# A Perceiver kernel's first cross attention: GpSimd's order within a key unit, values given out by half chunks, and scales spread at the end of the loop

## The chip, the cores and the metric

The kernel runs on one core of one Trainium2 chip (trn2). Its time is the device time of one execution in microseconds (us). Runs of one kernel are summed up by their median.

Engines are named as in the profile: PE is TensorE (matmul; PEld its weight loads), DVE is VectorE, ACT is ScalarE, POOL is GpSimd, SP is SyncE, which here only issues DMA transfers. An "L221" is line 221 of the kernel. Most instructions of the stage at issue carry that line, because a helper issues them, so they are told apart by the names of their tiles.

## The reference: what is computed

The reference is a network of four levels with twelve layers, each of the form `x = x + layer(layernorm(x))`, on `x` of 2 batches x 128 tokens x 256 channels. Only the first layer matters here, and of the tenth (the fourth level's cross attention) one tile pool. The first layer is a cross attention with int8-like fake quantisation:

```
q = layernorm(x) @ Wq + bq                  # 16 heads of 16 channels
k, v = split(ctx @ Wkv + bkv)               # ctx: 4096 tokens x 256 channels
q, k: quantised per token and head, scale = max|.| / 127
v: quantised per channel, scale = max|.| / 127 over all tokens
weights = softmax(q k^T / 4), quantised per row, scale = max / 255
x = x + (weights @ v) @ Wp + bp
```

The context of 4096 tokens is shared by both batches. In the kernel's code the softmax's weights are rounded to int16 by the conversion of an exponential, whose bias holds the maximum and log 255, and the row sums (`z`) divide the output at the end.

## The kernel before, in words

One program runs the twelve layers one after the other. The change concerns `l0_xattn` (from L316), which has a preparation and a loop. All its compute instructions go through `InOrder` (L213 to L221), which keeps each engine's instructions in the order in which the program names them. So the order of the work is written by hand: an engine never starts an instruction before those named earlier for it, and an instruction that waits holds up all behind it on its engine. DMA instructions stand in the queue of the engine that issues them.

**Loads.** ScalarE issues the loads of the key and value weights (`wkv`, one transfer), the query weights, the biases, and the output weights (L351 to L363); SyncE issues eight chunks of 512 context tokens, transposed (`ctxT`).

**Preparation** (a loop of ten steps `s`). Context tokens are 32 tiles of 128. Keys are made in eight units of four tiles (`Keys`). For a unit:

- `projected(0)` and `projected(2)`: TensorE projects two tiles each; VectorE adds the bias into `kn`.
- `scaled`: VectorE takes the maximum per token and head and the scale's reciprocal (`tr`, `kqr`); GpSimd multiplies `kn` by `kqr`. In the profile this is `kn<-kn,kqr`.
- `quantised`: ScalarE rounds to int16 (`kw<-kn`), VectorE multiplies by the scale (`kn<-kw,tr`).
- `first`: ScalarE casts the result to bf16 in the first third of `kpad`; GpSimd subtracts this part from `kn` (`kn<-kn,kpad`).
- `second`: ScalarE casts what is left to bf16 in the second third.
- `third`: GpSimd subtracts that too (`kpad<-kn,kpad`, the last third), and SyncE issues a DMA transpose of the unit's `kpad` into `kT` (L443).

So GpSimd has three operations for a unit: scaling, first, third. In step `s` the unit `s-2` does `second` and `third`, then unit `s-1` does `quantised` and `first`, then unit `s` does `scaled`. GpSimd's order in a step is therefore third(s-2), first(s-1), scaled(s).

Values are made transposed, in two halves of 128 channels (`Values(c)`), each in four chunks `n` of 1024 tokens, each of two half chunks `j`. TensorE projects a half chunk; ScalarE adds the bias and writes it to `vf` (`vf<-mm,bv`). VectorE takes the chunk's largest magnitude (`m<-vf`); after the fourth chunk the half's scale and its reciprocal (`vs`, `vr`) are known. `rounded(n)`: ScalarE rounds the chunk to int16 in `vws[n]`; `turned_values`: VectorE turns it into bf16 in place (`vw<-vw`), and SyncE issues a DMA transpose into `vi` (L347). There are four `vws` tiles, used by half 0 and again by half 1. One chunk is projected in each of steps 0 to 7: its first half chunk is copied out at once, its second in the next step (`late`).

`queries(b)` (ten VectorE instructions on small tiles and one transpose into `qT`) runs in steps 1 and 2 for the two batches.

**Loop** (`Round(h, b)`: 16 heads x 2 batches = 32 rounds). `scores(k)`: two matmuls of 512 keys into one of three PSUM tiles `sc`, from which VectorE copies to `S` with a running maximum (`S<-sc`). `weights`: VectorE makes the bias `nb`, ScalarE the rounded exponentials `Si` with their row sums (`Si<-S,nb,sq`), SyncE a DMA transpose into `pT`. `output(k)`: 8 matmuls into `po`, four rounds later (`LAG` = 4), so that in each turn of the loop TensorE does scores(k) of round n and output(k) of round n-4 by turns. There are two `S`, three `Si` and four `pT` tiles. The last round's exponentials are made in quarters, and its transposes are done on TensorE (`turned`, PSUM tiles `sc`, VectorE copies `pT<-sc`) rather than by DMA.

Before the loop, rounds 0 and 1 do scores 0 to 2; then half 1's values are turned; the bias `bp` is added to `x`; and the two rounds do scores 3 (which need `kT` of the last two units) and weights. Then `spread` of each half: VectorE makes a diagonal matrix of the value scales (`dg`), TensorE multiplies it with ones to give the scales in every partition (`sv`, one PSUM tile), ScalarE copies that to `svb`. `svb` is used only once, at the end, by the last product (L609).

In the tenth layer (L1333 on) the tile pool `l3kv` holds the norm weights and the tiles `kq`, `rot`, `v`. A tile pool that is opened on memory used by earlier tiles makes the first writers of its tiles wait for these; with `reuse_waits="tile"` each tile waits only for those that lay in its own place.

Of the kernel before, what the change touches and what calls it, by code (L numbers as in the profile page):

```python
# [12 lines left out]
F32 = mybir.dt.float32  # L13
# [4 lines left out]
AF = mybir.ActivationFunctionType  # L18
ALU = mybir.AluOpType
# [3 lines left out]
P = 128  # L23
B = 2
D = 256
# [290 lines left out]
def l0_xattn(g):  # L316
# [8 lines left out]
    nc, tc = g.nc, g.tc  # L325
# [3 lines left out]
    UP = 2.0 ** 64  # L329
    with ExitStack() as ctx:  # L330
        p1 = ctx.enter_context(tc.tile_pool(name="l0x", bufs=1, reuse_waits="tile"))
        pe, dve, act, pool = (InOrder(tc, e) for e in (nc.tensor, nc.vector, nc.scalar, nc.gpsimd))
# [6 lines left out]
        svb = p1.tile([P, D], F32, name="svb")  # L339
# [3 lines left out]
        def turned_values(c, n):  # L343

            vb = vws[n].bitcast(BF16)
            dve.tensor_scalar(vb, vws[n], UP, None, ALU.mult)
            nc.sync.dma_start_transpose(out=vi[:, 8 * n:8 * n + 8, c * P:(c + 1) * P], in_=vb)  # L347

        with tc.tile_pool(name="ctx0", bufs=1, reuse_waits="tile") as pc, tc.tile_pool(name="l0p", bufs=2, reuse_waits="tile") as p2, g.psum():
            ctxT = pc.tile([P, 2, NK], F32, name="ctxT0")  # L350
            wkv = pc.tile([P, 2, 2 * D], F32, name="wkv")  # L351
            nc.scalar.dma_start(wkv, g.ins["L0_xattn_Wkv"])
            wq = pc.tile([P, 2, D], F32, name="wq")
            nc.scalar.dma_start(wq, g.ins["L0_xattn_Wq"])
            bk = pc.tile([P, D], F32, name="bk")
# [1 line left out]
            bv = pc.tile([P, 2], F32, name="bv")  # L357
# [3 lines left out]
            nc.scalar.dma_start(wp, g.ins["L0_xattn_Wp"])  # L361
            bp = p1.tile([P, D], F32, name="bp")
            nc.scalar.dma_start(bp, g.ins["L0_xattn_bp"].partition_broadcast(P))  # L363
            for n in range(8):
                nc.sync.dma_start(ctxT[:, :, n * 512:(n + 1) * 512], g.ins["ctxT"][n])
            kpads = []
            for i in range(2):
# [19 lines left out]
            def queries(b):  # L387

                ps = g.acc()
                for c in range(2):  # L390
                    pe.matmul(ps, lhsT=xnT[:, c, b * P:(b + 1) * P], rhs=wq[:, c, :], start=(c == 0), stop=(c == 1))
                q = p2.tile([P, 16, 16], F32, tag="q16", name="q16", bufs=1)
                dve.tensor_tensor(q, ps.rearrange("p (h d) -> p h d", d=16), bq.rearrange("p (h d) -> p h d", d=16), ALU.add)
                dve.tensor_scalar(q, q, 0.25, None, ALU.mult)
                s, r = sq[:, b], g.sm([P, 16], "fqr")
                dve.tensor_reduce(s, q, AX.X, ALU.max, apply_absolute_value=True)
                dve.tensor_scalar(s, s, 1.0 / 127.0, 1e-8, ALU.mult, ALU.max)
                dve.reciprocal(r, s)
                dve.tensor_tensor(q, q, r.unsqueeze(2).to_broadcast([P, 16, 16]), ALU.mult)
                dve.tensor_scalar(nsq[:, b], s, -1.0, None, ALU.mult)  # L400
                for i in range(3):
                    dve.tensor_scalar(qpads[b][:, :, 16 * i:16 * i + 16], q, MAGIC, MAGIC, ALU.add, ALU.subtract)
                nc.sync.dma_start_transpose(out=qT[:, b], in_=qpads[b].rearrange("p h k -> p (h k)"))

            class Keys:
# [23 lines left out]
                def quantised(self):  # L429
# [15 lines left out]
            class Values:  # L445
# [7 lines left out]
                def projected(self, n, j):  # L453

                    if j == 0:
                        self.vf.append(p2.tile([P, 1024], F32, tag="vf", name="vf", bufs=4))
                    k0 = 1024 * n + 512 * j
                    ps = g.mm()
                    for k in range(2):
                        pe.matmul(ps, lhsT=wkv[:, k, D + self.c * P:D + (self.c + 1) * P], rhs=ctxT[:, k, k0:k0 + 512], start=(k == 0), stop=(k == 1))  # L460
                    return lambda: act.activation(self.vf[n][:, 512 * j:512 * j + 512], ps, AF.Identity, bias=bv[:, self.c:self.c + 1])

                def largest(self, n):
                    dve.tensor_reduce(self.m4[:, n:n + 1], self.vf[n], AX.X, ALU.max, apply_absolute_value=True)
# [5 lines left out]
                    dve.tensor_scalar(s, s, 1.0 / 127.0, 1e-8, ALU.mult, ALU.max)  # L470
                    dve.reciprocal(self.r, s)

                def spread(self, dg, ps):

                    dve.tensor_scalar(dg, g.ident, self.s, 2.0 ** 133 / UP, ALU.mult, ALU.mult)
                    pe.matmul(ps, lhsT=g.ones, rhs=dg, start=True, stop=True)
                    act.copy(svb[:, self.c * P:(self.c + 1) * P], ps)

                def rounded(self, n):
                    act.activation(vws[n], self.vf[n], AF.Copy, scale=self.r)  # L480

            vals, units, late = [Values(0), Values(1)], [], None

            when = {n + 4 * c: (c, n) for c in range(2) for n in range(4)}
            for s in range(8 + 2):
                now = Keys(s) if s < 8 else None
                one = units[s - 1] if 0 <= s - 1 < 8 else None
                two = units[s - 2] if s >= 2 else None
                if two:
                    two.second()  # L490
                    two.third()
                if late:
                    late()
                    late = None
                if now:
                    units.append(now)
                    now.projected(0)
                if one:
                    one.quantised()
                    one.first()  # L500
                if now:
                    now.projected(2)
                    now.scaled()
                if s - 1 in when:
                    c, n = when[s - 1]
                    vals[c].largest(n)
                if s in when:
                    c, n = when[s]
                    if c == 1:
                        vals[0].rounded(n)  # L510
                    vals[c].projected(n, 0)()
                    late = vals[c].projected(n, 1)
                    if c == 1:
                        turned_values(0, n)
                if s == 0:
                    turned_queries()
                if 1 <= s < 1 + B:
                    queries(s - 1)
            for n in range(4):
                vals[1].rounded(n)  # L520

        with tc.tile_pool(name="l0s", bufs=2, reuse_waits="tile") as p2, tc.tile_pool(name="l0ps", bufs=1, space=PSUM, reuse_waits="tile") as pp:
# [63 lines left out]
            for now in rounds:  # L586
                now.scores(3)
                now.weights(False)
            for v in vals:
                v.spread(p2.tile([P, P], F32, tag="dg", name="dg"), pp.tile([P, P], F32, tag="sv", name="sv", bufs=1))  # L590
            for n in range(2, len(todo) + LAG):
                now = Round(*todo[n]) if n < len(todo) else None
                rounds.append(now)
                if n == len(todo) + 1:
                    for k in range(4):
                        rounds[len(todo) - 1].turned(k)
                for k in range(4):
# [735 lines left out]
def l3_xattn(g, ctxT, cos, sin):  # L1333
# [10 lines left out]
    SCALE = float(np.float32(1.0 / np.sqrt(HD)))  # L1344
    pe, dve, pp = nc.tensor, nc.vector, None
    with ExitStack() as ctx:
        pk = ctx.enter_context(tc.tile_pool(name="l3kv", bufs=1))
        qw = pk.tile([P, HD], F32, name="qw")
        nc.sync.dma_start(qw, g.ins["L3_xattn_q_norm_w"].partition_broadcast(P))
        kw = pk.tile([P, HD], F32, name="kw")  # L1350
# [861 lines left out]
```

## Time and profile before

| what | us |
|---|---|
| runs of this kernel | 1601.31, 1607.47, 1612.97 |
| median | 1607.47 |
| the profiled execution's own time | 1609.98 |
| its span (first to last instruction) | 1608.3 |
| mean granted TensorE clock in the span | 0.89 |
| first matmul of the preparation | 8.60 |
| first and last scaling of a key unit on GpSimd, start | 16.62, 78.00 |
| last transpose into `kT`, issue | 88.85 |
| round 2's first `S<-sc` | 107.80 |
| last `S<-sc` of round 31, start | 258.46 |
| end of the outputs (`o<-po,z`, start) | 270.12 |

Views of the profile used below: the busy time of each engine in stretches of the span, with the clock that TensorE was granted as a share of full speed; the chain of work that ended last, followed back from the end (start, duration, engine, tile, and how many pieces were put together); the waits, by the engine that sat idle and by the work that released it (total, times, longest); and the timeline of an engine (start, duration, operation, output and inputs, and in brackets the idle time just before it with its releaser). SPq is SyncE's queue of DMA issues; the time of one issue there is how long it holds the queue, and its data land later. A line of instructions with "x8" and three durations gives the shortest, the median and the longest in ns.

### The profile page before, as it was taken

How to read it: one execution, taken by the hardware profiler on the slowest of the kernel's cores; microseconds unless marked ns; L12 is line 12 of the kernel's file. 1: busy time of each engine (PE TensorE's matmuls, PEld its weight loads, DVE VectorE, ACT ScalarE, POOL GpSimd, SP SyncE). 2: the span in 40 equal slices, each digit the busy share in tenths (PEclk: the TensorE clock that was granted, in tenths of full speed). 3: DMA queues.
4: the chain of work that ended last, by engine and by line, in shares of the span. 5: the costliest groups of instructions: out<-in, count | busy, mean ns of one | idle time of the engine just before them, and what ended most of it. 6: DMA issues, size and time to landing. Idle time of an engine off the chain costs nothing.

```text
span 1608.3 us, 17969 instructions
## 1 busy us (share of the span) xinstructions
PE 1444.2 (90%) x6732; PEld 908.3 (56%) x6732; DVE 1135.4 (71%) x1975; ACT 822.1 (51%) x1275; POOL 148.7 (9%) x140
## 2 busy tenths in 40 slices
PE   7759997898869999859999999999978999999978
PEld 5413334666546777636566566566544566666667
DVE  6869996485446476564765765765826899999976
ACT  3657775323213412315455455455546788888822
POOL 6710002020000000000000000000000111111110
PEclk9955555799979998769999999999999999999999
DMA  6889999734230430100000000000105122221110
GB/s 180 155 153 204 203 206 178 240 106 144 69 115 14 113 94 14 36 7 0 14 1 14 14 1 14 1 1 1 34 26 236 51 101 102 101 102 44 34 33 7
DMA packets 205615, 127.06 MB, mean 79 GB/s; under 512 B 177192, under 2 KB 184632, under 8 KB 202200
## 3 DMA queue, kind: packets, MB, share of 16 engines
q1 hardware_dynamic: 202720, 123.97, 30.2%
q10 hardware_dynamic: 2744, 1.76, 0.4%
q8 instruction: 53, 0.87, 0.2%
q14 instruction: 34, 0.28, 0.1%
q0 software_dynamic: 64, 0.18, 0.0%
HBM read 81.93 MB, written 0.26 MB: 51 GB/s over the span
## 4 chain that ended last, share of the span: by engine, by line
PE 73%; DVE 14%; ACT 7%; DMA 2%; issue 2%; POOL 1%; SPq 0%; ACTq 0%; DVEq 0%; POOLq 0%
PE mm L221 14%; PE wide L221 12%; PE mm L178 7%; PE py L221 7%; PE sc L221 6%; PE pb L221 6%; PE tr L221 4%; PE po L221 2%; PE acc L1147 2%; PE acc L221 2%; PE one L221 1%; DVE S L221 1%; DVE ro L221 1%; PE acc L1361 1%; DVE bc L221 1%
## 5 line engine op out<-in xcount | busy, mean ns | idle before, releaser
L221 DVE TENSOR_SCALAR_CACHE_REDUCE S<-sc 128x1024 f32<-128x1024 f32 x128 | 150.2, 1219 | 11.5 <-PE sc L221 11.0
L221 PE MATMUL py<-pT,v 128*128 128x512 f32 x272 | 142.5, 609 | 5.0 <-ACT pT L1476 4.9
L221 ACT ACTIVATE Si<-S,nb,sq 128x4096 int16<-128x4096 f32 (+1 forms) x35 | 122.7, 3506 | 46.2 <-issue 28.2
L221 PE MATMUL sc<-kT,qT 48*128 48x512 bf16 x256 | 130.6, 615 | 15.5 <-DMA kT<-kpad 6.4
L221 PE MATMUL wide<-kT,qT 128*128 128x512 f32 x256 | 120.7, 601 | 3.7 <-ACT v L1397 3.7
L1476 ACT COPY pT<-tr 128x512 f32<-128x512 f32 x136 | 78.5, 588 | 82.5 <-PE tr L221 82.5
L1465 ACT ACTIVATE S<-S,nb 128x2176 f32<-128x2176 f32 x32 | 67.5, 2108 | 94.3 <-DVE nb L221 94.3
L221 PE MATMUL pb<-wb,xT 128*128 128x512 f32 x256 | 112.6, 593 | 0.0
L221 DVE TENSOR_SCALAR_CACHE_REDUCE S<-wide 128x1024 f32<-128x1024 f32 x64 | 78.3, 1224 | 47.6 <-PE wide L221 47.2
L221 PEld LDWEIGHTS tr<-ident,S 128*128 128x128 f32 x544 | 68.4, 142 | 72.1 <-issue 43.4
L221 PE MATMUL wide<-w,ctxT 128*128 128x256 f32 x448 | 101.3, 379 | 0.0
L221 PEld LDWEIGHTS <-pT 128*128 128x128 bf16 x1024 | 36.5, 106 | 94.0 <-issue 89.4
L221 PEld LDWEIGHTS wide<-w,ctxT 128*128 128x128 f32 x448 | 83.0, 190 | 10.1
L221 PE MATMUL tr<-ident,S 128*128 128x128 f32 x544 | 81.9, 276 | 3.5 <-ACT S L1465 3.3
L221 PEld LDWEIGHTS pb<-wb,xT 128*128 128x128 f32 x256 | 48.9, 191 | 59.9 <-issue 56.4
L221 PEld LDWEIGHTS wide<-kT,qT 128*128 128x128 f32 x256 | 46.0, 190 | 58.0 <-issue 35.2
L221 DVE COPY kq<-wide 128x512 f32<-128x512 f32 (+1 forms) x42 | 26.3, 625 | 68.1 <-PE wide L221 64.6
L221 ACT ACT_TABLE_LOAD x53 | 68.0, 1283 | 3.7 <-PE mm L221 3.0
L221 ACT ACTIVATE bc<-pb,rs 128x128 f32<-128x128 f32 x256 | 68.2, 437 | 0.9 <-DVE rs L221 0.9
L221 ACT ACTIVATE bc<-pb 128x1024 f32<-128x1024 f32 x32 | 32.8, 1025 | 63.5 <-PE pb L221 63.5
L221 PE MATMUL mm<-m,xb 128*64 128x128 f32 x512 | 60.2, 275 | 2.9 <-DVE m L221 1.9
L221 PEld LDWEIGHTS mm<-m,xb 128*64 128x64 f32 x512 | 55.4, 137 | 6.7 <-DVE m L221 2.6
(533 smaller groups left out, 2924.3 us busy)
## 6 DMA issues: line engine op xcount, KB each, us to landing
w<-in_L_ffn_w_dram SPq DMA_DIRECT2D x25, 384.0 KB
ctxT<-in_ctxT_dram SPq DMA_DIRECT2D x16, 512.0 KB
wb<-in_L_attn_WB_dram SPq DMA_DIRECT2D x8, 1024.0 KB
wb<-in_L_attn_WC_dram SPq DMA_DIRECT2D x8, 1024.0 KB
bb<-in_L_attn_BC_bias_dram SPq DMA_DIRECT2D x8, 1024.0 KB
w<-in_ctx_dram SPq DMA_DIRECT2D x8, 512.0 KB
cx<-in_ctx_dram SPq DMA_DIRECT2D x8, 512.0 KB
wt<-in_L_attn_Wth_dram SPq DMA_DIRECT2D x8, 512.0 KB
```

Of the source, the lines that this page charges most:

```text
L178: self.nc.tensor.matmul(out, lhsT=lhsT(c), rhs=w(c), start=(c == 0), stop=(c == n - 1))
L221: return lambda *a, **k: self.tc.keep_in_program_order(f(*a, **k))
L1147: nc.tensor.matmul(acc[c], lhsT=kf[:, i, c * P:(c + 1) * P], rhs=cx[:, t % 4 + i, :], start=(t + i == 0), stop=(t + i == NT - 1))
L1361: pe.matmul(out, lhsT=lhsT(c), rhs=w[:, c, :], start=(c == 0), stop=(c == 1))
L1465: nc.scalar.activation(Sf, Sf, AF.Exp, bias=nm, scale=SCALE, accum_out=self.rz[:, r:r + 1])
L1476: nc.scalar.copy(pT, tp)
```

## The change

In the preparation of the first attention:

- `wkv` is loaded in two transfers, key weights and value weights; context chunk 0 in two transfers of 256 tokens.
- In a step, unit `s-2` does `second` at the start. Then the values whose half chunks were projected in the step before are copied out on ScalarE. Then unit `s` does both projections and `scaled`, then unit `s-2` `third`, and then unit `s-1` `whole` (the old `quantised`, renamed) and `first`. GpSimd's order is scaled(s), third(s-2), first(s-1). In the two last steps, with no unit `s`, third comes after first.
- Values are given out by half chunks: 1, 1, 2, 2, 2, 1, 2, 2, 2 and 1 in the ten steps, each copied out in the step after. `rounded` and `turned_values` of half 0 are in steps 5 to 8 and 6 to 9; the largest magnitude is taken when a chunk's second half chunk has been copied out.
- `turned_queries` is in step 1, the two `queries` in steps 5 and 6.
- `spread` is gone from the place before the loop. Its two diagonal matrices, two matmuls (into one PSUM tile of both halves) and one copy are in the loop at the turn after the last round's scores (`n == len(todo)`), before output(28) on TensorE, and on VectorE after the instructions of the last round's weights, the sum `z` of the four quarters among them.

In the tenth layer, the tile pool `l3kv` gets `reuse_waits="tile"`.

```diff
-            nc.scalar.dma_start(wkv, g.ins["L0_xattn_Wkv"])
+            for c in range(2):
+                nc.scalar.dma_start(wkv[:, :, c * D:(c + 1) * D], g.ins["L0_xattn_Wkv"][:, :, c * D:(c + 1) * D])
...
-            for n in range(8):
+            for j in range(2):
+                nc.sync.dma_start(ctxT[:, :, j * 256:(j + 1) * 256], g.ins["ctxT"][0, :, :, j * 256:(j + 1) * 256])
+            for n in range(1, 8):
                 nc.sync.dma_start(ctxT[:, :, n * 512:(n + 1) * 512], g.ins["ctxT"][n])
...
-                    return lambda: act.activation(self.vf[n][:, 512 * j:512 * j + 512], ps, AF.Identity, bias=bv[:, self.c:self.c + 1])
+
+                    def held():
+                        act.activation(self.vf[n][:, 512 * j:512 * j + 512], ps, AF.Identity, bias=bv[:, self.c:self.c + 1])
+                        return (self.c, n) if j else (None, n)
+
+                    return held
...
-                def spread(self, dg, ps):
-
-                    dve.tensor_scalar(dg, g.ident, self.s, 2.0 ** 133 / UP, ALU.mult, ALU.mult)
-                    pe.matmul(ps, lhsT=g.ones, rhs=dg, start=True, stop=True)
-                    act.copy(svb[:, self.c * P:(self.c + 1) * P], ps)
...
-            when = {n + 4 * c: (c, n) for c in range(2) for n in range(4)}
-            for s in range(8 + 2):
+
+            vals, units, late = [Values(0), Values(1)], [], []
+            parts = iter([(c, n, j) for c in range(2) for n in range(4) for j in range(2)])
+            for s, count in enumerate((1, 1, 2, 2, 2, 1, 2, 2, 2, 1)):
                 now = Keys(s) if s < 8 else None
                 one = units[s - 1] if 0 <= s - 1 < 8 else None
                 two = units[s - 2] if s >= 2 else None
                 if two:
                     two.second()
-                    two.third()
-                if late:
-                    late()
-                    late = None
+                done = [f() for f in late]
+                late = []
                 if now:
                     units.append(now)
                     now.projected(0)
-                if one:
-                    one.quantised()
-                    one.first()
-                if now:
                     now.projected(2)
                     now.scaled()
-                if s - 1 in when:
-                    c, n = when[s - 1]
-                    vals[c].largest(n)
-                if s in when:
-                    c, n = when[s]
-                    if c == 1:
-                        vals[0].rounded(n)
-                    vals[c].projected(n, 0)()
-                    late = vals[c].projected(n, 1)
-                    if c == 1:
-                        turned_values(0, n)
-                if s == 0:
+                    if two:
+                        two.third()
+                if one:
+                    one.whole()
+                    one.first()
+                if two and not now:
+                    two.third()
+                for c, n in done:
+                    if c is not None:
+                        vals[c].largest(n)
+                if 0 <= s - 5 < 4:
+                    vals[0].rounded(s - 5)
+                if s == 1:
                     turned_queries()
-                if 1 <= s < 1 + B:
-                    queries(s - 1)
+                for _ in range(count):
+                    c, n, j = next(parts)
+                    late.append(vals[c].projected(n, j))
+                if 0 <= s - 6 < 4:
+                    turned_values(0, s - 6)
+                if 5 <= s < 5 + B:
+                    queries(s - 5)
+            for f in late:
+                c, n = f()
+                vals[c].largest(n)
...
-            for v in vals:
-                v.spread(p2.tile([P, P], F32, tag="dg", name="dg"), pp.tile([P, P], F32, tag="sv", name="sv", bufs=1))
             for n in range(2, len(todo) + LAG):
                 now = Round(*todo[n]) if n < len(todo) else None
                 rounds.append(now)
+                if n == len(todo):
+
+                    sv = pp.tile([P, B, P], F32, name="sv")
+                    for c in range(2):
+                        dg = p2.tile([P, P], F32, tag="dg", name="dg")
+                        dve.tensor_scalar(dg, g.ident, vals[c].s, 2.0 ** 133 / UP, ALU.mult, ALU.mult)
+                        pe.matmul(sv[:, c, :], lhsT=g.ones, rhs=dg, start=True, stop=True)
+                    act.copy(svb, sv.rearrange("p c k -> p (c k)"))
...
-        pk = ctx.enter_context(tc.tile_pool(name="l3kv", bufs=1))
+        pk = ctx.enter_context(tc.tile_pool(name="l3kv", bufs=1, reuse_waits="tile"))
```

More of the change, by code (lines that the diff above doesn't have):

```diff
@@ L427, in scaled, with whole @@
                     pool.tensor_tensor(self.kn, self.kn, r.unsqueeze(2).to_broadcast([P, 64, 16]), ALU.mult)
-                def quantised(self):
+                def whole(self):
                     kw = p2.tile([P, 64, 16], I16, tag="kw", name="kw", bufs=1)
@@ L471, in largest @@
                     dve.reciprocal(self.r, s)
-                def spread(self, dg, ps):
-                    dve.tensor_scalar(dg, g.ident, self.s, 2.0 ** 133 / UP, ALU.mult, ALU.mult)
-                    pe.matmul(ps, lhsT=g.ones, rhs=dg, start=True, stop=True)
-                    act.copy(svb[:, self.c * P:(self.c + 1) * P], ps)
                 def rounded(self, n):
                     act.activation(vws[n], self.vf[n], AF.Copy, scale=self.r)
-            vals, units, late = [Values(0), Values(1)], [], None
-            when = {n + 4 * c: (c, n) for c in range(2) for n in range(4)}
-            for s in range(8 + 2):
+            vals, units, late = [Values(0), Values(1)], [], []
+            parts = iter([(c, n, j) for c in range(2) for n in range(4) for j in range(2)])
+            for s, count in enumerate((1, 1, 2, 2, 2, 1, 2, 2, 2, 1)):
                 now = Keys(s) if s < 8 else None
```

## The prediction

> **What bounds the kernel now.** I read the clock of each stage first, then the chain that ended last over the first 180 us, then GpSimd's timeline at the end of the preparation, the waits there, and the timeline of the loop's end. Only first attention changes its order (span 0 to about 272 us), so only that is costed, and one tile pool used from 651 us.
>
> The chain of work that ended last, start, us, what:
>
> ```profile
> 72.46 1.05 ACT kw L221
> 73.54 1.23 DVE kn L221
> 74.79 1.05 ACT kpad L221
> 75.92 1.62 POOL kn L221
> 78.00 1.93 POOL kn L221
> ...
> 88.85 6.81 DMA kT<-kpad
> 96.32 1.24 DVE S L221 x2
> ...
> 101.73 3.97 ACT Si L221 x3
> 106.70 0.98 PE sc L221 x2
> 107.80 4.68 DVE S L221 x8
> ```
>
> The preparation is a closed chain through four engines, not GpSimd alone: scaling on GpSimd 1.93, `kw` on ScalarE 1.05, dequantising on VectorE 1.23, the cast to `kpad` 1.05, the first subtraction on GpSimd (2.13 in the timeline), then the next unit's scaling. With gaps that is 7.5 us a unit (GpSimd's first subtractions start at 60.89, 68.41, 75.92). GpSimd's third operation (2.31) lies beside ScalarE and VectorE. After the last scaling (78.00) come `kT`'s last transpose (88.85) and the first round's last scores (96.32).
>
> Waits between 8 and 110 us (engine, line, releaser: total, times, longest), and then GpSimd's timeline (start, us, operation, idle time before it and its releaser):
>
> ```profile
> POOL kn L221 <- ACT kpad L221: 19.3, 8, 4.4
> ...
> DVE S L221 <- PE sc L221: 11.0, 2, 7.8
> ...
> PE sv L221 <- ACT svb L221: 5.3, 1, 5.3
> ```
> ```profile
> 79.89 2.30 POOL L221 TENSOR_TENSOR kpad<-kn,kpad 128x1024 bf16<-128x1024 f32 x1
> 83.42 2.12 POOL L221 TENSOR_TENSOR kn<-kn,kpad 128x1024 f32<-128x1024 f32 x1 [1.22 <-ACT kpad L221]
> 86.69 2.13 POOL L221 TENSOR_TENSOR kpad<-kn,kpad 128x1024 bf16<-128x1024 f32 x1 [1.15 <-ACT kpad L221]
> ```
>
> GpSimd waits 19.3 us for ScalarE, so its order alone can't shorten the chain. At the loop's start the second spread matmul waits 5.3 us for a ScalarE copy that stands behind two exponentials; round 2's scores stand behind it on TensorE, and VectorE waits 7.8. Busy time by stage (window, length, then each engine's busy us and its instructions, granted clock, DMA share, GB/s):
>
> ```profile
> 120.00:260.00 140.00, 139.59 (x1121) 46.51 (x1120) 137.71 (x278) 107.02 (x56) 0.95 (x1) 0.50 1.15 204
> ```
>
> In the loop TensorE, the first number, is busy 139.59 of 140 us at a granted clock of 0.50: four score pairs and outputs at 1.28, so 5.12 us a round; VectorE, the third, needs about 5.0. What delays the loop's start passes to its end whole.
>
> **The change, part by part.** I laid out each engine's queue in the built order with its waits, by these rows' durations. The same layout of the old kernel puts the last `kT` issue at 88.6 (traced 88.85), round 2's scores at 107.1 (107.80), the end of the outputs at 269.0 (270.12); differences below are layout against layout.
>
> Loads. Context chunk 0 and the weights come in halves, two more DMAs on SyncE's and ScalarE's queues. TensorE waited 8.6 us for the weights (landed 8.47). Their size suggests about 8.0; bounds −1.5 to +1.5. The extra issue on ScalarE is ahead of its table load and the layer norm on VectorE, which precedes the first key addition (12.76). That addition, not TensorE, sets the first scaling: 16.5 for 16.0. I take +0.5.
>
> Order on ScalarE. The second cast of unit s−2 waits for its first subtraction on GpSimd. It stands ahead of one or two value copies (0.69 each) and of `kw` for unit s−1. GpSimd now scales unit s first, does third(s−2), and only then first(s−1). So scaling leaves the chain (−1.93), but the second cast (+1.05) and one or two value copies (+0.6 to 1.2 overlapped) enter: 1.05 + 1.2 + 1.05 + 1.23 + 1.05 + 2.13 + 0.1 of handoffs = 7.8 with two copies, 7.2 with one; before 7.5. The expected shortening is not there. Scalings start at 16.5, 20.6, 26.5, 34.1, 41.6, 49.6, 61.8, 73.7: the first two steps are short because scaling of unit 1 no longer waits for first(0).
>
> Queries move from steps 1 and 2 to 5 and 6. Their VectorE operations took 4.5 and 5.0 (25.34 to 29.87, 35.40 to 40.42). In both kernels they stand ahead of additions, but now the dequantising of unit s−1 comes after unit s's additions and reciprocal. The chain of such a step: query 4.5, additions 1.3, reduction, maximum and reciprocal 2.1, dequantising 1.2, then scaling and third on GpSimd ahead of first: 12 a step against 10.5. Sum over seven steps: 57.2, before 61.8. The last scaling is thus 4.1 earlier (73.7; layout before 77.8).
>
> Tail. After scaling 7 the old path needs 10.85 us to the last `kT` issue. The new: scaling 1.93, third(5) 2.13, first(6) 2.13 plus 0.5 of blocking, second cast 1.05, two copies 1.2, `kw` 1.05, dequantising 1.2, cast 1.05, first(7) 2.4, third(6) 2.13, third(7) 2.13 = 18.9, to 92.5. Here `kT`(6) is issued only at 90.5 (82.22 before), behind first(7), and a transpose holds SyncE 4.82: `kT`(7) issues at 95.4, +6.8, lands at 102.2.
>
> A new wait. Value transpose (0,3) stands on SyncE's queue behind both: issue 100.3, landing 103.6. ScalarE's rounding of (1,3) reuses that `vws` tile and waits; VectorE's conversion, the two additions to `x` and the last scores of rounds 0 and 1 stand behind it. First such scores 105.8 for 96.0: +9.8.
>
> Loop start. Spread leaves it; −5.3 is VectorE's gap that goes: round 2's scores start when the first exponential frees its tile, 111.6 for 107.1: +4.5.
>
> Loop end. The timeline before:
>
> ```profile
> 265.26 0.16 DVE L221 TENSOR_REDUCE z<-z 128x1 f32<-128x4 f32 x1 [5.12 <-ACT Si L221]
> ...
> 268.21 1.87 PE L221 MATMUL po<-vi,pT 128*128 128x16 bf16 x64 [0.18 <-DMA pT<-Si]
> ```
>
> The two `dg` (about 0.3; at the old place 0.47 for both) stand on VectorE behind the `z` reduction, which waits for all four exponential quarters (265.42). Both spread matmuls wait for `dg`, and output(28) and the four transposes of round 31 stand behind them on TensorE; output(28) and three transposes had been hidden under the exponentials. From 265.4: 0.3 + spread 1.5 (0.80 each, overlapped) + output 0.93 + transposes 4 × 0.88 + three outputs 2.8 = 9.05; before 4.7 (270.12). +4.3. Sum: +4.5 + 4.3 = +8.8.
>
> Two rules weighed. Row: the loop's TensorE is busy throughout and granted 0.50, as shown. The Trainium skill, "TensorE: Matmul & The Clock Gate", Part 1, says that about 3.4 us of sustained work release the full clock. By the rule the loop-end cost halves to about 2.4, and the loop would run at VectorE's 5.0; by the row it is 4.3. I take the row. Second, the conversion of values: VectorE took 0.42 alone and up to 1.75 beside GpSimd:
>
> ```profile
> L221 DVE TENSOR_SCALAR vw<-vw x8: 420/424/1748, 55.3 to 92.0; 128x1024 bf16<-128x1024 int16 x8
> ```
>
> "SBUF — State Buffer", "Who interferes with whom", makes the block last the whole of the other's instruction. That speaks against queries placed where GpSimd is busiest: by the rule +8.8, with blocks capped at 1.3 (the row's excess) +8.1, with none +7.5. I take +8.4.
>
> The tile pool at 651 us. The key copy and a square there wait for fewer semaphores. The trace shows VectorE going on 0.34 us behind `x`, and ScalarE waiting for VectorE's copy, so little can go: 0 to −0.8, and it costs nothing as it only removes waits. I take −0.3.
>
> Sum: +8.1. Against the profiled execution's 1609.98 (span 1608.3) 1618.1; against the runs' median of 1607.47, 1615.6, say 1616.
>
> **Rivals.** Own case (0.66): 1609 to 1623.
>
> A, not slower (0.13): ScalarE's second cast and copies don't hold `kw` back, GpSimd falls toward its busy sum 1.93 + 2.13 + 2.13 = 6.2, the queries hide. From 16.5, five steps of 6.2 and two of 9 give 65.5; with the old tail of 10.85 and queue waits `kT`(7) issues at about 78, 10 earlier. Less the spread's 5.3, plus 4.3, plus 3 for the value wait: about −8, 1599. For it: 19.3 us of GpSimd's waiting, and TensorE's work would permit 69. Against: the second cast stands ahead in ScalarE's own order. With `kT`(7) delayed by d the sum is d + 3.0 − 5.3 + 4.3 = d + 2.0; it decides where `kT`(7) issues before about 86.8, some 8 earlier than laid out.
>
> B (0.05): preparation and gain at the start cancel, only the loop's end stays: about 1612, or, with clock above 0.50 there, 1607. Then the change does nothing that can be measured.
>
> C (0.16): worse. TensorE idles over 3 us between query steps and falls to half clock (before, 8 matmuls after such a gap took 5.24 for 3.60), further blocking, and a transpose queue that is late for rounds 0 to 3: each 1.6 to 5, together +16 or more, 1624 to 1630.
>
> **How the numbers follow.** One measurement of this kernel tells about 1% from no change (runs 1601 to 1613): the bounds are 1591 and 1624. From 1616, the range reaches down over B and most of A, and up over part of C: 1602 to 1626. Faster 0.06 (A's far half), slower 0.20 (C, and the own case's edge), same 0.74.
>
> **What would show it.** GpSimd's waits for ScalarE stay near 15 us or more; its period between steps 2 and 5 is 7.5 to 8; two steps of 12 with queries; `kT`(6) issues right ahead of `kT`(7) near 90 and 95; ScalarE's last value rounding waits for a value DMA; round 2's scores no longer wait for spread; output(28) starts after the last exponential. It is wrong if the period is 6.2, or if the loop's granted clock leaves 0.50.

## The result and the profile after

The changed kernel takes 1616.44 us (median of 20 runs, 1605.06 to 1627.92), the kernel before 1608.66 (20 runs, 1597.24 to 1613.91): ratio 1.0061, 95% interval 1.0040 to 1.0082, so 6 to 13 us slower. The profiled execution has a span of 1612.3 us.

In that execution the product of `po` and `z`, which ends first attention, starts at 279.55 instead of 270.12: +9.4. The forecast laid out +8.8 and took +8.4. Behind it lie 1321 to 1339 us in the 14 executions profiled here, before and after and all experiments, without order; the after one happens to have 5 less there than the before one. So the stage is read by this product's start, and the whole by the medians.

The chain that ended last, after (start, us, what), answers the chain shown for before:

```profile
30.00 7.34 DMA kT<-kpad
37.42 1.05 ACT kpad L221
...
73.16 1.93 POOL kn L221
75.09 2.09 POOL kpad L221
77.18 2.27 POOL kn L221
79.44 6.29 issue
85.77 2.13 POOL kn L221
...
100.52 3.23 DMA vi<-vw
103.83 1.16 ACT vw L221
106.10 1.15 DVE S L221 x2
...
111.65 4.68 DVE S L221 x8
```

The last scaling (73.16) is 4.8 earlier than before's 78.00, but first(6), its successors up to first(7) and the third operations follow one after another. Then a DMA of values, not of keys, is what the chain goes through: ScalarE's last rounding starts when `vi` has landed. Round 2's scores start 3.9 later than before's 107.80.

The waits between 8 and 112 us, after:

```profile
POOL kn L221 <- DVE kqr L221: 21.6, 8, 5.8
...
POOL kn L221 <- ACT kpad L221: 8.8, 5, 6.3
...
ACT vw L221 <- DMA vi<-vw: 6.5, 1, 6.5
...
ACT kpad L221 <- DMA kT<-kpad: 4.2, 2, 2.2
```

and one line of the same view before:

```profile
POOL kn L221 <- DVE kqr L221: 4.5, 1, 4.5
```

GpSimd waited 19.3 us for ScalarE's cast before, and 4.5 for VectorE's reciprocal. Now it waits 8.8 and 21.6: not less than before, only elsewhere. The last line after has no counterpart before: ScalarE's first cast of a unit now waits for a transpose (experiment 9). The loop's row by stage shows the same clock, 0.50, and TensorE nearly as busy:

```profile
120.00:260.00 140.00, 138.77 (x1089) 45.71 (x1088) 136.86 (x275) 105.81 (x56) 0.00 (x0) 0.50 1.15 203
```

The loop's end, after, in order of time:

```profile
269.35 2.52 POOL L633 TENSOR_SCALAR_AFFINE_SELECT ex<-ex 16x2816 bf16<-16x2816 bf16 x1
...
270.46 0.16 DVE L221 TENSOR_REDUCE z<-z 128x1 f32<-128x4 f32 x1 [5.12 <-ACT Si L221]
270.53 1.62 DVE L221 TENSOR_SCALAR dg<-ident,vs 128x128 f32<-128x128 f32 x2
...
272.01 1.22 PE L221 MATMUL sv<-dg,ones 128*128 128x128 f32 x4 [8.07 <-DVE dg L221]
...
273.02 1.05 PE L221 MATMUL po<-vi,pT 128*128 128x16 bf16 x32
...
273.92 3.21 PE L221 MATMUL sc<-identb,Si 128*128 128x128 bf16 x32
...
276.96 2.55 PE L221 MATMUL po<-vi,pT 128*128 128x16 bf16 x96
279.55 0.69 DVE L618 TENSOR_TENSOR o<-po,z 128x512 f32<-128x512 f32 x1 [1.58 <-PE po L221]
```

TensorE idles 8.07 us for `dg`. Output(28) and three of the four transposes stood under the exponentials before and are now behind it: from the `z` reduction to the product 9.09 us, before 4.86.

### The profile page after: what moved, and what is told of

It reads as the page before. It is cut to its first block, busy times and chain, and to the rows that moved or that the text cites. A ratio compares the mean times of both kernels' runs of the same rounds, so it can differ in the third digit from the quotient of the medians.

```text
span 1612.3 us, 17977 instructions
## 1 busy us (share of the span) xinstructions
PE 1441.2 (89%) x6732; PEld 905.3 (56%) x6732; DVE 1136.7 (71%) x1975; ACT 821.1 (51%) x1274; POOL 149.8 (9%) x140
## 4 chain that ended last, share of the span: by engine, by line
PE 65%; DVE 19%; ACT 7%; DMA 4%; issue 3%; POOL 1%; SPq 0%; ACTq 0%; DVEq 0%; POOLq 0%
PE mm L221 13%; PE wide L221 12%; PE mm L178 7%; PE py L221 7%; DVE S L221 6%; PE pb L221 6%; PE tr L221 4%; PE acc L1158 2%; DMA pT<-Si 2%; PE one L221 1%; PE sc L221 1%; PE acc L221 1%; DVE bc L221 1%; PE acc L1372 1%; DVE kq L221 1%
## 5 line engine op out<-in xcount | busy, mean ns | idle before, releaser
L221 DVE TENSOR_SCALAR_CACHE_REDUCE S<-sc 128x1024 f32<-128x1024 f32 x128 | 150.6, 1219 | 3.7 <-ACT Si L221 2.4
```

Of the source, the lines that this page charges most:

```text
L221: return lambda *a, **k: self.tc.keep_in_program_order(f(*a, **k))
```

## The experiments

Executions differ in when the first loads land: with the loads in halves, TensorE's first matmul starts between 6.43 and 8.95. So each product start is also given less an offset, as if a late start were passed on whole: of the first scaling against 16.62 for kernels made from before, of the second scaling against 20.34 for those made from the changed kernel (experiments 3 and 7, whose second step differs: of the first against 16.77).

| kernel | product starts | less offset | against its parent | ratio of times to before, 95% interval |
|---|---|---|---|---|
| before | 270.12 | 270.1 | | 1 |
| changed | 279.55 | 279.6 | +9.4 | 1.0061, 1.0040 to 1.0082 |
| 1: before, spread at the loop's end | 270.85 | 270.2 | +0.1 | 1.0007, 0.9990 to 1.0025 |
| 2: before, GpSimd's new order (5 runs) | 284.13 | 283.0 | +12.9 | 1.0103, 1.0065 to 1.0142 |
| 3: changed, GpSimd's old order | 273.82 | 273.9 | −5.7 | 1.0004, 0.9981 to 1.0027 |
| 4: before, one `sv` tile, queries split | 265.38 | 264.0 | −6.2 | 0.9949, 0.9926 to 0.9973 |
| 5: changed, `kw` ahead of second cast | 279.48 | 277.1 | −2.5 | 1.0041, 1.0017 to 1.0065 |
| 6: changed, queries at steps 7 and 8 | 274.59 | 274.0 | −5.6 | 1.0035, 1.0013 to 1.0057 |
| 7: changed, queries at steps 1 and 2 | 281.48 | 281.5 | +2.0 | 1.0048, 1.0026 to 1.0070 |
| 8: changed, third(6) ahead of first(7) | 276.13 | 276.3 | −3.3 | 1.0042, 1.0017 to 1.0066 |
| 9: as 5, four `kn` tiles | 279.09 | 279.2 | −0.4 (to 5: +2.1) | one run |
| 10: changed, `vi` (0,3) a step earlier | 278.12 | 276.6 | −3.0 | one run |
| 11: before, one `sv` tile | 268.32 | 267.8 | −2.3 | 0.9970, 0.9946 to 0.9994 |
| 12: changed, one `sv` tile ahead of the loop | 277.88 | 277.0 | −2.5 | 1.0042, 1.0016 to 1.0068 |

In 5 the whole −2.5 is the offset. Up to 1.0 us of a difference between kernels with the spread at the loop's end can come from TensorE's clock there (last section).

My theory is the prediction's: the new order gains nothing per unit, lengthens the tail, and the moved spread is paid for at the loop's end. The rivals are that GpSimd's busy sum sets the pace (A), and that the loss is the queries' or the spread's.

**1. The spread alone.** The diff's two hunks in the loop part (`spread` out, the block at `n == len(todo)` in), nothing else.

> The kernel before with one part of the change: the spread of the value scales leaves the place before the loop and stands at the turn after the last round's scores. My theory: round 2's first scores on VectorE move from 107.8 to about 102.5 (-5.3: the wait for ScalarE's copy goes), and from the last exponential quarter to the product of po and z takes 9.1 instead of 4.9 (+4.2), so that product starts about 1 us earlier (269.1 for 270.12) and the time is within 0.3% of before. Rival, spread is free at the loop's end: -5.3 (264.8). Rival, the gap at the loop's start is not the spread's: no gain there, +4.2 (274.3).

The first scores of round 2 in this run, and its loop's end:

```profile
102.55 1.23 DVE L221 TENSOR_SCALAR_CACHE_REDUCE S<-sc 128x1024 f32<-128x1024 f32 x1 [2.38 <-ACT Si L221]
```
```profile
261.27 0.16 DVE L221 TENSOR_REDUCE z<-z 128x1 f32<-128x4 f32 x1 [5.12 <-ACT Si L221]
...
270.85 0.69 DVE L613 TENSOR_TENSOR o<-po,z 128x512 f32<-128x512 f32 x1 [1.70 <-PE po L221]
```

Less the offset of 0.66 the start gains 5.9. The end takes 270.85 − 261.27 = 9.6 for 4.9 and gives 4.7 back. The loop between gives back another 1.3 (150.66 before, 151.93 here, from round 2's first to round 31's last scores): both rivals fall, and the move is worth nothing (forecast −1; the loop's growth was not in it).

**2. GpSimd's order alone**, in the kernel before:

```diff
                 if two:
                     two.second()
-                    two.third()
...
-                if one:
-                    one.quantised()
-                    one.first()
                 if now:
                     now.projected(2)
                     now.scaled()
+                    if two:
+                        two.third()
+                if one:
+                    one.quantised()
+                    one.first()
+                if two and not now:
+                    two.third()
```

> The kernel before with GpSimd's order alone changed to scaled(s), third(s-2), first(s-1), with both projections of a unit ahead of the older unit's rounding; values, queries, loads and spread as before. My theory (the second cast of unit s-2 stands ahead of the rounding of unit s-1 on ScalarE and waits for GpSimd's first subtraction, so the chain is no shorter, and the last kT transposes come late behind first(7)): last scaling about 80.5 (before 78.0), kT(6) and kT(7) issued at about 97 and 102 (before 82.2 and 88.85), the product of po and z at about 283 (+13), time +13 us or 0.8%. Rival, GpSimd's period falls to its busy sum of 6.2 a unit: kT(7) issued before 80 and the time 8 us lower. Rival, the order is neutral and the loss lies in the values, queries and spread: within 2 us of before.

SyncE's queue in this run:

```profile
98.11 9.81 SPq L443 DMA_TRANSPOSE kT<-kpad  x2
```

The last scaling starts at 81.81 (80.7 less the offset), and the last two `kT` transposes are issued back to back from 98.11 (before: 82.22 and 88.85). The order alone costs 12.9 us of the stage and 1.0% of the time. It is not GpSimd's order only: the unit's second projection and VectorE's additions, maximum and reciprocal for it move ahead of the older unit's rounding too, here and in 3, and the two weren't separated. Rival A would have put `kT`(7) before 80.

**3. The order undone**, in the changed kernel (`third` behind `second`, `scaled` and the second projection behind `first`).

> The changed kernel with one part undone: GpSimd's order is third(s-2), first(s-1), scaled(s) again, with the second projection behind the older unit's rounding; half chunks, queries at steps 5 and 6, loads in halves and spread at the loop's end stay. My theory: the tail costs the old 11 us from last scaling to kT(7) (scaling about 77.5, kT(6) 82, kT(7) 89), round 2's scores at about 106, the product of po and z at about 273 (6.3 before the changed kernel's 279.55, 2.5 to 3 behind before's 270.12). Rival, the order doesn't matter: 279.5. Rival, the order helps and queries and spread hurt: later than 279.5.

Without the order 5.7 of the 9.4 are gone; the 3.7 that stay are less than the times can tell from before. Experiments 2 and 3 together: the order is the larger loss, 12.9 by itself. The rest of the change costs 3.7 without it and takes back 3.5 of it where both are there. Of that rest only the spread (1) and the queries' place (6, 7) were tried by themselves; the half chunks, the halved loads and the tile pool were not.

**5. What paces a step.** The changed kernel, ScalarE's rounding ahead of the second cast:

```diff
                     act.copy(kw, self.kn)
+                    if two:
+                        two.second()
                     dve.tensor_tensor(self.kn, kw, ...
```

(and `second` at the step's start, and `third` ahead of `first`, accordingly).

> The changed kernel with one edit on ScalarE: the rounding of unit s-1 (kw) stands ahead of the second cast of unit s-2, so it no longer waits for GpSimd's first subtraction. This tells whether that cast paces the steps. Strong form of my theory (only the cast paces): periods in steps 3 to 5 fall from 7.6 and 8.5 towards 6.2 to 6.5 and everything after is 4 us or more earlier. Weak form (with the cast gone TensorE's keys and values, busy 7.1 of 7.6 us in such a step, pace it): periods stay at 7.5, steps with queries and the tail give 1 to 2 us, the product of po and z at about 278.0 (after: 279.55). Rival, the cast isn't in the chain at all: 279.5 and the tail as after.

Scalings from 28.36 to 51.18 are 7.6 apart, as in the changed kernel. The second cast alone doesn't pace the steps: the strong form of my theory falls. The weak form had the period right and its cause, TensorE, wrong: the waits in these three steps show VectorE waiting for GpSimd.

```profile
DVE kn L221 <- POOL kpad L221: 5.9, 3, 2.0
```

There are three `kn` tiles. VectorE's additions for unit s+1 wait until GpSimd's third has freed the tile of unit s−2, and third now stands behind scaled(s): scaling 1.93 + third 2.13 + additions 1.29 + reduction, maximum and reciprocal 2.1 + handoffs 0.2 = 7.6, a second loop as long as the first. In the changed kernel it already holds the step from 25.95 to 33.57: VectorE's additions wait 0.3 us there for third(0).

**9. With a fourth `kn` tile** (`bufs=3` to `bufs=4`, and `svb` moved to the loop's tile pool to make room), on top of 5.

> The kernel of the run before (rounding ahead of the second cast) with four kn tiles instead of three (svb moves to the loop's pool to make room). The run before kept periods of 7.6, and its VectorE waited 2.0 us for GpSimd's third to free a kn tile. Theory (three loops lie close together: second cast 7.6, reuse of kn 7.6, TensorE's keys and values 7.1): with both gone the steps 2 to 4 fall to 7.1, TensorE's, and not to GpSimd's 6.2; VectorE no longer waits for GpSimd's third; the tail is as in the run before and the product of po and z within 1.5 us of it (279.5). Rival, GpSimd sets the pace once the tiles are there: periods of 6.2 to 6.5. Rival, something else holds the steps: 7.6 as before.

Scalings at 25.87, 32.76 and 40.05 are 6.9 and 7.3 apart, 7.1 in the mean as forecast, and between 26 and 50 us VectorE waits for TensorE and no longer for GpSimd's third:

```profile
ACT kpad L221 <- DMA kT<-kpad: 6.2, 2, 3.8
DVE kn L221 <- PE mm L221: 4.9, 5, 1.7
```

The 6.9 is TensorE's own pace: its matmuls follow one another without a gap there. The 7.3 is not. The first line shows another loop, which neither the prediction nor this expectation has. There are two `kpad` tiles, so ScalarE's first cast of unit u waits until the transpose of unit u−2 has read its tile, and the new order issues that transpose later. The cast at 36.84 waited 3.8 us, and first(2) and scaling 4 stand behind it. The cast at 43.55 waited 2.4, and the next step is 8.6 long (scaling at 48.60), because TensorE idles 1.8 us for a value copy that stands behind the cast at 36.84 on ScalarE. In the changed kernel the same wait, 2.2 us ahead of the cast at 37.42, is in the chain that ended last: by the rows around it about 0.9 of the 8.5 us between the scalings at 41.18 and 49.70. This loop is read from the waits; a third `kpad` tile was not tried.

So four limits lie close together: second cast 7.6, `kn` reuse 7.6, TensorE 6.9, and the transpose that frees `kpad`. GpSimd's 6.2 was out of reach in any order tried. The last scores of round 0 are at 103.31, but the product is no earlier than in the changed kernel: ScalarE's table load for the exponentials (1.28 us) now stands between `nb` and the first of them, and the loop's end took 9.6.

**6 and 7. The queries' place**, in the changed kernel: `queries(s - 7)` at steps 7 and 8; or `turned_queries` at step 0 and `queries(s - 1)` at steps 1 and 2.

> The changed kernel with the two queries at steps 7 and 8 instead of 5 and 6, where VectorE's queue has waits of 5.3 and 4.2 us. My theory: the steps of 12.2 and 11.3 become about 8.2 each (last scaling at about 66 instead of 73.2), but half 1's values and the tail of kT take half of it back: kT(7) at about 90.8 (95.2), last scores of round 0 about 101.4 (106.0), the product of po and z at about 274.8 (279.55, -4.7). Rival, a query costs the same wherever it stands: no change at the end. Rival, all 7.4 us of the two steps reach the end: 272.

> The changed kernel with the two queries (and their transposed input) back at steps 1 and 2 (0), as in the kernel before. My theory: the first steps lengthen to 9 to 11 us, the later ones stay at 7.5 to 8.5 and the last scaling is at about 75 (after 73.2), the values of half 1 come in the same steps; kT(7) at about 98 (95.2), the product of po and z at about 282 (+2.7): the queries' move alone was no loss. Rival, the queries' place is what costs the changed kernel its time: back to about 272 to 275.

With the queries at 7 and 8 the last scaling starts at 66.50, 6.7 earlier (7.3 less the offset), and 5.6 reach the product. At 1 and 2, the place before, the product is 2.0 later than in the changed kernel. So a query costs less where VectorE waits anyway (steps 7 and 8), and moving the queries to 5 and 6 was no loss against their old place. The times of these runs can't tell 2 us apart.

**8 and 10. The tail.** In 8, `third` stands ahead of `whole` and `first` in the steps without a unit `s`; in 10, `turned_values(0, 3)` comes in step 8 instead of 9.

> The changed kernel with one edit in the two last steps: third(6) stands ahead of first(7) on GpSimd, so kT(6) is issued before the last unit's first subtraction, as in the kernel before. My theory: kT(6) at about 84 (90.0), kT(7) at about 91.5 (95.2), last scores of round 0 at about 102.8 (106.0), the product of po and z at about 276.3 (-3.2). Rival, SyncE's queue isn't the limit there, the values of half 1 are: less than 1 us.

> The changed kernel with the last value transpose of half 0 a step earlier, ahead of kT(7) on SyncE's queue rather than behind it. My theory (ScalarE's last rounding into the same vws tile waits 6.5 us for that transpose, and the last scores of rounds 0 and 1 stand behind it): that wait goes, last scores of round 0 at about 103.5 (106.0), round 2's at 109.1 (111.65), product of po and z at about 277 (-2.6). Rival, kT(7) sets the last scores anyway: no change (kT(7) lands at about 102.5, scores at 105.5 or later).

SyncE's queue in 8:

```profile
83.25 4.87 SPq L446 DMA_TRANSPOSE kT<-kpad  x1
88.21 1.29 SPq L347 DMA_TRANSPOSE vi<-vw  x1
90.90 4.86 SPq L446 DMA_TRANSPOSE kT<-kpad  x1
```

`kT`(6) goes out at 83.25 instead of 90.00, the value transpose slips in between, and 3.3 us reach the product. In 10 ScalarE rounds its four chunks without a gap:

```profile
94.06 4.27 ACT L221 ACTIVATE vw<-vf,vr 128x1024 int16<-128x1024 f32 x4 [1.87 <-DVE vr L221]
```

The 6.5 us of waiting are gone and 3.0 reach the product: TensorE's last scores then wait for `kT`(7), 3.3 us. Both terms of the tail are shown, each by itself; together they weren't run.

**4, 11 and 12. The spread without its wait.** The spread stays ahead of the loop, both halves in one PSUM tile. As I placed the lines they are inside the loop over rounds 0 and 1, so the spread is done twice there, once behind each round's weights:

```diff
             for now in rounds:
                 now.scores(3)
                 now.weights(False)
-            for v in vals:
-                v.spread(p2.tile([P, P], F32, tag="dg", name="dg"), pp.tile([P, P], F32, tag="sv", name="sv", bufs=1))
+                sv = pp.tile([P, B, P], F32, name="sv")
+                for c in range(2):
+                    dg = p2.tile([P, P], F32, tag="dg", name="dg")
+                    dve.tensor_scalar(dg, g.ident, vals[c].s, 2.0 ** 133 / UP, ALU.mult, ALU.mult)
+                    pe.matmul(sv[:, c, :], lhsT=g.ones, rhs=dg, start=True, stop=True)
+                act.copy(svb, sv.rearrange("p c k -> p (c k)"))
```

> The kernel before with one edit: the spread at its old place, both halves into one PSUM tile with one copy. My theory: the second spread matmul waits for no copy, round 2's scores start at about 104.4 (107.8), the loop's end keeps its 4.9 us from the last quarter to the product of po and z, which starts at about 266.7 (-3.4), time -0.2%. Rival, VectorE's 7.8 us before round 2 is not this wait: no gain (270).

> The changed kernel with the spread back ahead of the loop, in one PSUM tile with one copy. My theory: from the z reduction to the product of po and z 4.9 us (changed kernel: 9.1), round 2's scores about 1.9 later than the changed kernel's 111.65 because the two matmuls stand there, sum -2.4: product of po and z at about 277.1, time still some 0.4% over before because the tail of the preparation stays. Rival, the loop's end is hidden by what follows: no change in time.

In 11 round 2's scores start at 105.34 (−3.0 less the offset) and the end takes 5.5: −2.3 at the product (forecast −3.4), 0.3% in time. In 12 the sum of −2.5 is the forecast one, its parts are not: the end takes 5.2 instead of 9.1 (−3.9 for −4.2), the start +2.8 for +1.9, the loop −1.4 for 0. Done once, it should save more; that wasn't run.

Number 4 adds the queries in two parts, on top of 11:

```diff
                 dve.tensor_reduce(s, q, AX.X, ALU.max, apply_absolute_value=True)
+                yield
...
                 nc.sync.dma_start_transpose(out=qT[:, b], in_=qpads[b].rearrange("p h k -> p (h k)"))
+                yield
...
-                if 1 <= s < 1 + B:
-                    queries(s - 1)
+                if 1 <= s < 1 + 2 * B:
+                    if (s - 1) % 2 == 0:
+                        asked = queries((s - 1) // 2)
+                    next(asked)
```

> The kernel before with two edits of mine: the spread stays where it was but uses one PSUM tile for both halves and one copy, so the second matmul waits for no copy; and each query's VectorE instructions are split after the first reduction over two steps (steps 1 to 4 rather than 1 and 2), so that half of them lie in VectorE's wait for the rounding. My theory: query steps of about 8 to 10 instead of 10.5, last scaling at about 74.3 (before 78.0), kT(7) at 85.1 (88.85), round 2's scores at about 100.6 (107.8), no loss at the loop's end: the product of po and z at about 263 (-7), time -0.4%. Rival, the chain is paced elsewhere and the start of the loop by transposes: no gain (270).

The scores of round 2:

```profile
102.87 1.22 DVE L221 TENSOR_SCALAR_CACHE_REDUCE S<-sc 128x1024 f32<-128x1024 f32 x1 [2.23 <-PE sc L221]
```

That is 6.4 earlier than before less the offset of 1.42. This version beats both kernels: 1599.94 us, 0.51% under before (interval 0.27 to 0.74%). At the product it gains 6.2 of the 7 that were forecast, 3.9 of them over 11.

## Why the prediction was right, point by point

The stage's sum: start of the loop +3.9 for +4.5, the loop itself +1.35 for nothing, its end +4.2 for +4.3; together +9.4 for +8.8. The direction and the two costs that carry it, tail and loop's end, were seen. That the sum lies so near is in part luck, as the points show.

- **Loads.** Wrong by about 1 us. TensorE began at 6.4 to 6.8 in seven of the nine executions with halved loads and at 8.2 and 9.0 in two (forecast 8.0), at 8.4 to 8.9 in the five with whole ones. The first scaling started at 16.72 in the middle one of those nine, at 17.28 in that of these five: −0.6 instead of +0.5.
- **The steps.** Scalings at 16.77, 20.34, 25.95, 33.57, 41.18, 49.70, 61.87 and 73.16, each within 0.6 of the forecast. Right in size and half right in cause: the prediction named one loop, and experiments 5 and 9 show four. Its first sign failed: GpSimd's waits for ScalarE were to stay near 15 us or more and fell to 8.8. The wait moved to VectorE's reciprocal, since scaling now comes first in GpSimd's step. The other signs came, the period with one step of 8.5 where 7.5 to 8 was forecast.
- **The tail.** From the last scaling to the end of third(7) 18.9 was forecast; the timeline has third(7) ending at 87.85 + 4.21 = 92.1, 18.9 behind 73.16. Two misses cancel in it: the last unit's cast waits for the transpose of unit 5 until 84.64, 0.7 behind the dequantising's end at 83.94, and the two first operations took 0.6 less than laid out. `vi` (0,3) was issued at 100.5 (100.3), the last scores of round 0 at 106.0 (105.8), round 2's at 111.65 (111.6). Experiments 8 and 10 each take one part of the delay away.
- **The loop.** Forecast: a delay passes to its end whole. It grew by 1.35 (152.01 for 150.66, round 2's first to round 31's last scores). This term was missing.
- **The loop's end.** +4.2 for +4.3, but by two errors that cancel. The two `dg` took 1.62, not 0.3. The work behind them took 7.5 (279.55 − 272.01), not 8.75: from start to start the spread took 1.0 for 1.5, the transposes 3.0 for 3.5, the three outputs 2.6 for 2.8. About 0.3 of this is the clock, which did not stay at 0.50 (last section); the rest is that matmuls follow one another more closely than the pieces that I added.
- **The tile pool in the tenth layer.** Forecast −0.3; the two traces are 5.68 apart at ScalarE's last table load ahead of that layer (592.85 before) and 5.62 at one within it (690.03): nothing to speak of.
- **Rivals.** A would show a period of 6.2; between steps 2 and 5 no run here goes below 6.9. B is near to what experiment 3 looks like, not the changed kernel. Of C, TensorE's clock did fall in the query steps (0.86 and 0.79), and the scalings still came when laid out.

The likeliest case was forecast at 1616 and measured at 1616.44; against the 20 runs of before the +8 is +7.8 by medians and +9.8 by the ratio. That the two figures agree to half a microsecond is luck: single runs of one kernel lie 23 us apart.

## What to carry to other kernels

When engines keep the program's order, moving an operation ahead takes it out of one loop of waits and puts what is passed into another: here the second cast, and the tiles that the third operation and the transpose behind it free. Write down every loop with its length, the reuse of tiles among them (a DMA that reads a tile counts), before expecting an engine's busy sum. Work that is moved from a wait at the start of a loop to its end is only free if something still covers it there; here an output and three transposes came out from under the exponentials. And look at the queue of transposes at the tail: one late transpose held up the next, and a rounding behind that.

## What the runs showed of the hardware that was not expected

**Blocked VectorE instructions** were longer than before's 1.75 us. One conversion of values took 2.32 us, beside a GpSimd third (0.42 alone):

```profile
L221 DVE TENSOR_SCALAR vw<-vw x8: 418/424/2324, 62.7 to 105.0; 128x1024 bf16<-128x1024 int16 x8
```

At the loop's end the first `dg` took 1.42 us (0.28 before, at its old place). It ended within 0.1 us of GpSimd's `affine_select` of the next layer: 269.35 + 2.52 = 271.87, as shown above. This is what the Trainium skill says in "SBUF — State Buffer", "Who interferes with whom": where an instruction of VectorE and one of GpSimd contend for the pair of ports that they share, the one that issues first keeps it to its end. The prediction's cap of 1.3 was too low, and the blocking work needn't be of the same layer.

**The loop** is 1.3 to 1.9 us longer whenever no spread stands ahead of it: 150.6 to 150.7 in the five kernels that have it (before, 2, 4, 11, 12), 151.9 to 152.5 in the other nine. In the after trace output matmuls wait for `pT` between 185 and 225 us; in before only their weight loads do (1.7 us, 4.8 after):

```profile
PE po L221 <- DMA pT<-Si: 1.2, 3, 0.7
```

One such transpose holds SyncE's queue 4.92 us (median); a round takes 5.01 early in the loop and 5.12 later. So a start that brings rounds 0 to 2 closer together leaves it little to catch up with. That the queue is the cause is argued from these rows and was not tried by itself.

**The clock.** From 120 to 260 us it was 0.50 in all 14 executions, with TensorE shown as busy for 95 to 99.7%, against the rule weighed in the prediction. At the loop's end it did not stay there. Where the spread stands there (nine kernels), TensorE idles some 8 us and then works without a gap, and the granted clock goes to 1.00 3.2 to 5.4 us after the spread's first matmul; after, at about 276.5, 4.5 us behind 272.01:

```profile
275.00:276.00 1.00, 1.00 (x12) 1.00 (x10) 0.87 (x2) 0.00 (x0) 0.00 (x0) 0.50 1.01 279
277.00:278.00 1.00, 1.00 (x45) 1.00 (x43) 0.97 (x2) 0.00 (x0) 0.00 (x0) 1.00 1.03 323
```

In the other five, where TensorE has gaps between the exponentials' quarters, it is 0.50 until the product. So the prediction's row held for the loop, and at the loop's end its rule did, roughly. The rule's halved cost did not follow: the 32 transposes took 3.04 us to the next matmul, 3.37 where the clock rose only behind them (1, 3 and 9) and 2.43 in 5, where it rose first, and the 96 output matmuls took 2.55 to 2.60 in all nine. Those transposes are most of why the loop's end took from 8.5 (7) to 9.6 us (1, 3 and 9). Why the loop's own matmuls don't release the clock stays open.
